# Two subtractions of the last pair's gate inputs move from GpSimd to VectorE

## The chip, the core and the metric

The kernel runs on one core of a Trainium2 chip. A core has a matrix engine (TensorE, PE in the profile; its weight loads are PEld), a vector engine (VectorE, DVE), an engine for activation functions (ScalarE, ACT), a general engine (GpSimd, POOL) and one that only issues transfers (SyncE, SP). Each works through its own instructions in the order in which they were written, and waits on semaphores for the others. Operands lie in SBUF; matmuls write their sums to the eight banks of PSUM, which the other engines read. The metric is the device time of one execution, in microseconds (us).

## What is computed

A gated graph layer on 32 graphs of 512 nodes with 256 features in float32. Cut to what matters here:

```python
h = relu(layernorm(x))
x_conv = relu(bn2(conv17(relu(bn1(conv1(h))))) + h)      # 17 taps along the nodes
x_nmp = (exp(-dist(s)) * adj) @ relu(h @ w_msg + b_msg)  # s: three features of h
gi = concat(x_conv, x_nmp) @ w_ih.T + b_ih
gh = h @ w_hh.T + b_hh
r, z = sigmoid(gi_r + gh_r), sigmoid(gi_z + gh_z)
n = tanh(gi_n + r * gh_n)
out = x + (1 - z) * n + z * h
```

So the three gates r, z and n need three products each, by h, by x_nmp and by x_conv (the sums of r and z can be made in one bank; those of n need h apart from the other two).

## The kernel before

The kernel first makes h, the convolution (by way of a transform along the nodes, with products in the transformed domain) and the messages x_nmp, and leaves them in DRAM. The change lies in the last stage, the gates, from about 815 us of the span on. The loop of this stage goes over 16 pairs of graphs, p = 0 to 15. The order of all instructions on all engines is that of the code (a manual schedule), so what the code writes first on an engine runs first on it.

**Operands of a pair.** HN[p] holds h and x_nmp of both graphs as [128, 2, 4, 512]: two sources and four rows, a row being one half of the features of one graph. CP[p] holds the convolution's rows as [128, 4, 512]; `inverse(p)` (line 870) makes it by PE (line 878), DVE (line 884) and ACT (line 886). The text says "hn" for the first two sources and "c" for the convolution.

**Products.** The gates' matrix products are made by schemes that trade products for sums, so PE is fed with differences of rows. For pairs 0 to 14 the gates r and z go by a scheme of 26 products of 256 columns (`gates_rz26`, line 889, matmuls on line 915), and n by one of seven products of 512 columns (`gate_n`, line 1048). For the last pair, 15, r and z too go by seven products (`gates_rz`, line 939, for r; `last_z`, line 984, for z). All matmuls of the schemes of seven are on line 932. Seven products are named Q1 to Q7 and stand in the order Q1, Q6, Q2, Q7, Q5, Q4, Q3. Each takes one operand:

```python
[plain[B11], r5, plain[B21], t3, t4, r6, plain[B22]]     # Q1, Q6, Q2, Q7, Q5, Q4, Q3 take 0, 1, 2, 3, 4, 5, 6
```

with t4 = row 1 - row 0, r5 = row 3 - t4, t3 = row 3 - row 1, r6 = row 2 - r5 (`PAIR_SUMS`). Each of these has two hn parts (tiles tn, line 812, two instructions) and a c part (tile tnc, line 814, one instruction of 128 x 512). Q6 thus multiplies r5: first its two hn parts, then its c part.

**Where the differences are made.** They are made by GpSimd in `block_sum` (line 795), except for two c parts of the first pair, t4 and r5, which VectorE makes. For the last pair, `sums(15, True)` (line 820) lists t4, r5, t3, r6, each hn before c, and is called behind `gate_n(14)`. On GpSimd they stand behind four weight sums of `load_last` (line 844).

**gate_n and what follows it on VectorE.** In `gate_n(14)`, `finished` (line 1063) reads a product's banks and makes the input of a tanh by four steps of VectorE (lines 1071 to 1074), and `blend` (line 1138) makes the gated result by three steps of VectorE: h - n (reads PSUM), times z (both inputs in SBUF), plus n (reads PSUM). In the profile the steps of the first blend have line 1102, of the second line 1110 and of the last two line 1061. Near its end `gate_n` reads:

```python
        finished(x3, u3, x1, 1, 1)
        pair(Q4, x2, False)
        finished(x2, p1, x2, 1, 0)
        if not last:
            for step in blend(p, 1, 1):
                step()
        pair(Q3, x3, False)
        late = finished(x3, u2, x3, 0, 1, not last)
```

Then comes the last pair's `gates_rz`. ScalarE copies Q1's bank (p1, line 957), VectorE adds it to Q6's bank (u2, line 962), Q7 is added by PE onto that same bank, and VectorE makes u3 from it (line 971); the results come from line 950. The third and fourth blend of pair 14 stand between these.

Of the kernel before, what the change touches and what calls it, by code (L numbers as in the profile page):

```python
# [91 lines left out]
FIRST_ORDER = (  # L92
    ('t4', 'hn'), ('r5', 'hn'), ('E5', 'hn'), ('t3', 'hn'), ('E9', 'hn'), ('E4', 'hn'), ('E8',
    'hn'), ('E0', 'hn'), ('E6', 'hn'), ('t4', 'c'), ('r5', 'c'), ('E5', 'c'), ('t3', 'c'), ('E9',
    'c'), ('E4', 'c'), ('E8', 'c'), ('E0', 'c'), ('E6', 'c'), ('E7', 'hn'), ('E7', 'c'), ('E2',
    'hn'), ('E2', 'c'), ('r6', 'hn'), ('r6', 'c'), ('E1', 'hn'), ('E1', 'c'), ('E3', 'hn'), ('E3',
    'c'),
)
HALFWAY = 12
WEIGHT_SUMS = (  # L100
    '3=a+b', '9=a-c', '4=b+9', '5=d-4', '19=a+g', '6=b+19', '8=h+6', '11=f+9', '20=e+g', '26=f+h',
# [61 lines left out]
def gnn_layer(  # L163
# [15 lines left out]
    nc = tc.nc  # L179
    B, N, D = x.shape  # L180
# [21 lines left out]
    def bank(name):  # L202
        return psum.tile([P, N], FP, tag="bank", name=name)
# [502 lines left out]
    def combine_weights():  # L706

        steps, loads, begins = [], [], []
        for k, src in enumerate((w_hhT, w_ihT[D:], w_ihT[:D])):
# [26 lines left out]
            for n, (dst, x1, x2, op) in enumerate(((Q5, n21, n22, ALU.add), (Q6, q[Q5], n11, ALU.subtract),  # L736
# [4 lines left out]
                if n == 1:  # L741
                    steps[-1].append(partial(nc.sync.dma_start, WH[:, k, :HALFWAY], u[:, :HALFWAY]))
                if n == 0 and k > 0:
                    begins.append(len(steps) - 1)
            steps[-1].append(partial(nc.sync.dma_start, WN[:, k], t))
            steps[-1].append(partial(nc.sync.dma_start, WH[:, k, HALFWAY:], u[:, HALFWAY : len(PRODUCTS)]))
        steps[0].append(loads[0])
# [14 lines left out]
    def shared(name):  # L762
        return pools["yn"].tile([P, 2, len(spans) + 1, D], FP, tag="yn", name=name, bufs=1)
# [14 lines left out]
    def operand(p, name, part):  # L778

        if name[0] == "b":  # L780
            row, cols = place(name)
            return CP[p][:, row, cols] if part == "c" else HN[p][:, :, row, cols]
        if name[0] == "E":
            n = EXTRA.index(name)
            return TEC[0][:, n] if part == "c" else TE[0][:, n]
        row, h = list(PAIR_SUMS).index(name[:2]), int(name[3])
        cols = slice(HALF * h, HALF * h + HALF)
        return TNC[0][:, row, cols] if part == "c" else TN[0][:, row, :, cols]
# [3 lines left out]
                               (TEC, "tec", [len(EXTRA), HALF]), (RZ, "rz", [2 * DC, 2, N]), (CT, "ct", [6, N])):  # L792
            t[0] = pools[name].tile([P, *shape], FP, tag=name, name=name, bufs=1)

    def block_sum(p, name, part):
        if name in BLOCK_SUMS:
            x, op, y = BLOCK_SUMS[name]
            dst, x, y = (operand(p, v, part) for v in (name, x, y))
            op = ALU.add if op == "+" else ALU.subtract
        else:  # L800
            rows = list(PAIR_SUMS)

            def whole(v):
                if isinstance(v, int):
                    return CP[p][:, v] if part == "c" else HN[p][:, :, v]
                return TNC[0][:, rows.index(v)] if part == "c" else TN[0][:, rows.index(v)]

            (x, y), op = PAIR_SUMS[name], ALU.subtract
            dst, x, y = whole(name), whole(x), whole(y)
            if part == "hn":  # L810
                for k in range(2):
                    nc.gpsimd.tensor_tensor(dst[:, k], x[:, k], y[:, k], op=op)  # L812
                return
        (nc.vector if p == 0 and (name, part) in FIRST_ORDER[ahead : ahead + 2] else nc.gpsimd).tensor_tensor(dst, x, y, op=op)

    def sums_ahead(p, part):
        for name in SUMS_AHEAD:
            block_sum(p, name, part)

    def sums(p, last):  # L820
        for name, part in [(name, part) for name in PAIR_SUMS for part in ("hn", "c")] if last else SUM_ORDER:
            block_sum(p, name, part)

    def load_combined(s0, s1):
        if "hk" not in SW:
# [23 lines left out]
    def load_pair_x(p):  # L849

        XP[p] = []
        for b in (2 * p, 2 * p + 1):
            t = pools["xb"].tile([P, N // 32, D // 4], FP, tag="x", name=f"xb_{b}", bufs=2)
            for g in range(4):
                nc.sync.dma_start(t[32 * g : 32 * (g + 1)], quarter(x[b], g))
            XP[p].append(t)
# [72 lines left out]
    def into(bk, q, o, ks, terms, first, t=slice(0, N)):  # L929

        for i, k in enumerate(ks):
            nc.tensor.matmul(bk[:, t], weight(q, k, o), terms[k][q][:, t], start=(first and i == 0), stop=(i == len(ks) - 1),  # L932
                             skip_group_check=True)

    def temp(role, name):
        n = TURN[role] = TURN.get(role, 1) + 1
        return CT[0][:, 2 * ("u3", "p1", "u2").index(role) + n % 2, :]
# [110 lines left out]
    def gate_n(p, terms, last, old=None):  # L1048
        rz, o = RZ[0], 2
        t = shared(f"nt_{p}").rearrange("p j c d -> p (j c d)")  # L1050
        NT[p] = nt = t[:, : DC * 2 * N].rearrange("p (i j n) -> p i j n", i=DC, j=2)
        h, i_ = [0], [1, 2]
        add, mul = ALU.add, ALU.mult

        def pair(q, banks, first):
            for bk, ks in zip(banks, (h, i_)):
                into(bk, q, o, ks, terms, first)

        def run(steps):
            for step in steps:  # L1060
                step()

        def finished(banks, other, spare, i, j, later=False):

            n, r = nt[:, i, j, :], rz[:, i, j, :]
            (bk, bk_i), (h, g) = banks, spare
            if other is None:
                nc.vector.scalar_tensor_tensor(n, bk, b_hn[:, i : i + 1], r, op0=add, op1=mul)
                nc.vector.tensor_add(n, n, bk_i)
            else:  # L1070
                nc.vector.scalar_tensor_tensor(h, bk, b_hn[:, i : i + 1], other[0], op0=add, op1=add)
                nc.vector.tensor_mul(n, h, r)
                nc.vector.tensor_add(g, other[1], bk_i)
                nc.vector.tensor_add(n, n, g)  # L1074
            NEW[p, i, j] = n if last else g
            tanh = partial(nc.scalar.activation, NEW[p, i, j], n, AF.Tanh, bias=b_in[:, i : i + 1], scale=1.0)
            return tanh if later else tanh()  # L1077

        if last:
            old(0)  # L1080
        x1 = [bank(f"pn1_{p}_{k}") for k in range(2)]
        pair(Q1, x1, True)
        p1 = [temp("p1", f"n{p}_{k}") for k in range(2)]
        for k in range(2):
            nc.scalar.copy(p1[k], x1[k])
        x2 = [bank(f"pn2_{p}_{k}") for k in range(2)]
        pair(Q6, x2, True)
        u2 = [temp("u2", f"n{p}_{k}") for k in range(2)]
        for k in range(2):
            nc.vector.tensor_add(u2[k], p1[k], x2[k])  # L1090
        if last:
            old(1)
            load_pair_x(p)
        pair(Q2, x1, False)
        finished(x1, None, x1, 0, 0)
        pair(Q7, x2, False)
        u3 = [temp("u3", f"n{p}_{k}") for k in range(2)]
        for k in range(2):
            nc.vector.tensor_add(u3[k], p1[k], x2[k])
        if not last:  # L1100
            for step in blend(p, 0, 0):
                step()
        x3 = [bank(f"pn3_{p}_{k}") for k in range(2)]
        pair(Q5, x3, True)
        finished(x3, u3, x1, 1, 1)
        pair(Q4, x2, False)
        finished(x2, p1, x2, 1, 0)
        if not last:
            for step in blend(p, 1, 1):
                step()  # L1110
# [3 lines that stand above are left out]
            rest = partial(run, blend(p, 1, 0)), partial(run, blend(p, 0, 1))  # L1114
            if p + 2 < B // 2:
                rest[0]()
                rest = rest[1:]
            return late, *rest
        if last:
            for i, j in ((0, 0), (1, 1), (1, 0), (0, 1)):  # L1120
                nc.gpsimd.tensor_tensor(rz[:, i, j, :], HN[p][:, 0, 2 * i + j, :], nt[:, i, j, :], op=ALU.subtract)
                if j == 0:
                    early_out(p, i, j)
# [14 lines left out]
    def blend(p, i, j):  # L1138
        n, d = NEW.pop((p, i, j)), RZ[0][:, i, j, :]
        return [partial(nc.vector.tensor_tensor, d, HN[p][:, 0, 2 * i + j, :], n, op=ALU.subtract),  # L1140
                partial(nc.vector.tensor_tensor, d, d, RZ[0][:, DC + i, j, :], op=ALU.mult),
                partial(nc.vector.tensor_tensor, NT[p][:, i, j, :], d, n, op=ALU.add)]
# [322 lines left out]
    with phase(*homes), tc.manual_schedule():  # L1465
# [8 lines left out]
        ahead = [v[1] for v in FIRST_ORDER].index("c")  # L1474
        for name, part in FIRST_ORDER[:ahead]:
            block_sum(0, name, part)
# [3 lines left out]
        for p in range(pairs):  # L1480
# [7 lines left out]
            if more:  # L1488
                last = p + 2 == pairs
# [63 lines left out]
```

## Time and profile before

| What | Value |
|---|---|
| median of 4 runs | 1732.99 us (1730.87 to 1736.97) |
| profiled execution, its own time | 1731.53 us |
| its span, first to last instruction | 1729.8 us |
| TensorE busy | 1715.0 us, 99% |
| VectorE busy | 1303.5 us, 75% |
| GpSimd busy | 1085.7 us, 63% |
| mean granted clock of TensorE | 0.999 |

The rows of a timeline are: start in us from the span's start, length in us, engine, line, operation, tile written <- tiles read, shapes, count; in brackets the engine's idle time before it and what ended it. A row with x4 merges four instructions. A float32 matmul shows as two rows on PE, so a 512-column product with three terms has six: four for its hn terms and two for its c term. The name pg is a bank of the r and z gates, pn of the n gate, pz of the last pair's z gate; ct is the tile of the temporaries p1, u2 and u3, rz holds r and z, nt the n gate.

### The profile page before, as it was taken

The page shows a single profiled execution, that of the slowest core. Times are in us where ns is not written, and L with a number is a line of the kernel's source. Part 1 is how long each engine was busy: PE and PEld are TensorE (multiplying, and loading weights), DVE is VectorE, ACT ScalarE, POOL GpSimd, SP SyncE. Part 2 cuts the span into 40 slices and gives each one's busy share as a digit, 9 for nine tenths or more (in the row PEclk, how much of TensorE's full clock was granted, in tenths as well). Part 3 has the DMA queues.
Part 4 walks back from the last instruction along what each step waited for, and adds up shares of the span by engine and source line. Part 5 has one row for each costly group of instructions (what it writes and reads, how often), then busy time and mean ns, then how long its engine had stood idle before and what let it go on. Part 6 is the DMA issues. An engine that isn't in the chain of part 4 may idle for free.

```text
span 1729.8 us, 24317 instructions
## 1 busy us (share of the span) xinstructions
PE 1715.0 (99%) x7920; PEld 1320.4 (76%) x7920; DVE 1303.5 (75%) x2599; ACT 691.4 (40%) x1669; POOL 1085.7 (63%) x1074
## 2 busy tenths in 40 slices
PE   9999999999999999999999999999999999999998
PEld 6767888888998888887877778777877787778744
DVE  7875877777996677666587778777887778777867
ACT  4556655553446555554323232232323232323221
POOL 3331777687655677777767657665667556755551
PEclk9999999999999999999999999999999999999999
DMA  9989988885778888798433454335523553335433
GB/s 260 297 281 259 264 234 243 253 232 178 269 250 230 267 242 244 230 257 305 119 103 74 80 128 112 75 71 128 128 69 64 124 128 88 78 90 128 108 57 73
DMA packets 311681, 295.07 MB, mean 171 GB/s; under 512 B 147436, under 2 KB 241164, under 8 KB 311172
## 3 DMA queue, kind: packets, MB, share of 16 engines
q1 hardware_dynamic: 301588, 265.17, 56.4%
q0 software_dynamic: 6960, 26.65, 4.8%
q10 hardware_dynamic: 3008, 1.72, 0.3%
q8 instruction: 63, 1.03, 0.3%
q14 instruction: 62, 0.51, 0.1%
HBM read 194.31 MB, written 99.16 MB: 170 GB/s over the span
## 4 chain that ended last, share of the span: by engine, by line
PE 89%; DVE 4%; DMA 2%; SPq 2%; issue 1%; POOL 1%; ACT 0%; DVEq 0%; POOLq 0%
PE pg L915 27%; PE pn L932 15%; PE py L503 11%; PE pn L670 10%; PE pm L558 6%; PE pc L439 5%; PE pc L878 3%; PE px L454 3%; PE pd L608 2%; PE phT L419 1%; PE pw L363 1%; PE pz L932 1%; PE pg L932 1%; PE pn L653 1%; PE pc L881 1%
## 5 line engine op out<-in xcount | busy, mean ns | idle before, releaser
L470 POOL TENSOR_TENSOR wsum<-wt 128x512 f32<-128x512 f32 x66 | 94.1, 1426 | 101.6 <-DMA wt<-wd 67.3
L503 PE MATMUL py<-wt,xf 128*128 128x256 f32 x640 | 154.2, 384 | 0.0
L915 PE MATMUL pg<-te,sw 128*128 128x256 f32 x600 | 154.0, 379 | 0.0
L906 ACT ACTIVATE rz<-rz,brz 128x256 f32<-128x256 f32 x180 | 86.2, 504 | 147.0 <-DVE rz L921 146.9
L503 PEld LDWEIGHTS py<-wt,xf 128*128 128x128 f32 x640 | 117.1, 190 | 34.9 <-issue 20.5
L915 PEld LDWEIGHTS pg<-te,sw 128*128 128x128 f32 x600 | 114.0, 190 | 15.5
L915 PE MATMUL pg<-hn,sw 128*128 128x256 f32 x480 | 123.2, 379 | 0.0
L915 PE MATMUL pg<-tn,sw 128*128 128x256 f32 x480 | 123.2, 379 | 0.0
L618 DVE TENSOR_TENSOR A<-A,at 128x512 f32<-128x512 f32 x124 | 115.9, 974 | 6.3 <-ACT A L614 2.7
L932 PE MATMUL pn<-tn,sw_n 128*128 128x512 f32 x256 | 120.3, 592 | 0.0
L1077 ACT ACTIVATE pn<-nt,vech 128x512 f32<-128x512 f32 x45 | 31.1, 692 | 218.7 <-DVE nt L1074 139.4
L439 PE MATMUL pc<-w,hT 128*128 128x256 f32 x512 | 117.7, 383 | 0.7 <-DVE hT L423 0.7
L558 PE MATMUL pm<-wmsg,hq 128*128 128x259 f32 x512 | 117.3, 381 | 0.0
L439 PEld LDWEIGHTS pc<-w,hT 128*128 128x128 f32 x512 | 94.6, 190 | 23.8 <-issue 6.4
L812 POOL TENSOR_TENSOR tn<-hn 128x512 f32<-128x512 f32 x64 | 86.3, 1369 | 35.7 <-PE pn L932 35.6
L558 PEld LDWEIGHTS pm<-wmsg,hq 128*128 128x128 f32 x512 | 96.5, 189 | 14.6
L915 PEld LDWEIGHTS pg<-hn,sw 128*128 128x128 f32 x480 | 91.1, 190 | 18.3 <-PE pn L932 3.3
L915 PEld LDWEIGHTS pg<-tn,sw 128*128 128x128 f32 x480 | 91.2, 190 | 12.4
L921 DVE TENSOR_TENSOR ct<-pg,ct 128x256 f32<-128x256 f32 x180 | 74.8, 415 | 32.9 <-PE pg L915 23.5
L932 PEld LDWEIGHTS pn<-tn,sw_n 128*128 128x128 f32 x256 | 48.6, 190 | 61.2 <-issue 50.9
L932 PE MATMUL pn<-hn,sw_n 128*128 128x512 f32 x192 | 90.3, 592 | 0.0
L915 PE MATMUL pg<-tec,sw 128*128 128x256 f32 x300 | 89.2, 379 | 0.0
(236 smaller groups left out, 4328.0 us busy)
## 6 DMA issues: line engine op xcount, KB each, us to landing
wt<-wd SPq DMA_DIRECT2D x80, 512.0 KB, 6.5
adj<-in_adj_dram SPq DMA_DIRECT2D x128, 256.0 KB, 5.9
wd<-wst SPq DMA_DIRECT2D x64, 320.0 KB, 5.3
yd<-y SPq DMA_DIRECT2D x76, 256.0 KB, 5.0
hd<-hT SPq DMA_DIRECT2D x32, 512.0 KB, 4.7
nd<-nmp SPq DMA_DIRECT2D x32, 512.0 KB, 2.9
xb<-in_x_dram SPq DMA_DIRECT2D x128, 128.0 KB, 6.4
out_dram<-xb SPq DMA_DIRECT2D x122, 128.0 KB, 2.8
```

The source lines that it names most:

```text
L439: nc.tensor.matmul(p[:, j, :], HT[b][:, ic, c * P : (c + 1) * P], w1[:, ic, :], start=(ic == 0), stop=(ic == DC - 1))
L454: nc.tensor.matmul(p[:, j * 2 * L : (j + 1) * 2 * L], H1[b][:, c0 + j, ic * P : (ic + 1) * P], fwd, start=True, stop=True)
L470: nc.gpsimd.tensor_tensor(t, WT[g, u][:, 0], WT[g, u][:, 1], op=ALU.add)
L503: nc.tensor.matmul(dst, v[:, ic, :], w[:, ic, :], start=(ic == 0), stop=(ic == DC - 1))
L558: nc.tensor.matmul(p[:, : D + NS], hq[:, ic, c * P : (c + 1) * P], wmsg[:, ic, :], start=(ic == 0), stop=(ic == DC - 1))
L618: nc.vector.tensor_mul(A[b][:, mc, :], EXP.pop((b, mc)), AT.pop((b, mc)))
L670: nc.tensor.matmul(bk, left[:, k, :], right[:, k, :], start=(first and k == 0), stop=(k == 1), skip_group_check=True)
L812: nc.gpsimd.tensor_tensor(dst[:, k], x[:, k], y[:, k], op=op)
L906: nc.scalar.activation(at(dst), at(src), AF.Sigmoid, bias=brz[:, o : o + 1], scale=sign)
L915: nc.tensor.matmul(bk, SW["hk"][:, k, s, :], c if k == 2 else hn[:, k], start=(onto is None and k == 0), stop=(k == K3 - 1), skip_group_ch ...
L921: nc.vector.tensor_tensor(at(dst), at(x), at(y), op=op)
L932: nc.tensor.matmul(bk[:, t], weight(q, k, o), terms[k][q][:, t], start=(first and i == 0), stop=(i == len(ks) - 1), skip_group_check=True)
```

## The change

The c parts of t4 and r5 of the last pair are made by VectorE instead of GpSimd. They are issued in `gate_n(14)`, behind the `finished` of Q4 and ahead of the second blend (line 1110). `sums(15, True)` leaves them out. The hn parts, t3 and r6 stay on GpSimd in their order.

```diff
+EARLY_SUMS = (("t4", "c"), ("r5", "c"))
...
-    def block_sum(p, name, part):
+    def block_sum(p, name, part, engine=nc.gpsimd):
...
-        (nc.vector if p == 0 and (name, part) in FIRST_ORDER[ahead : ahead + 2] else nc.gpsimd).tensor_tensor(dst, x, y, op=op)
+        if p == 0 and (name, part) in FIRST_ORDER[ahead : ahead + 2]:
+            engine = nc.vector
+        engine.tensor_tensor(dst, x, y, op=op)
...
     def sums(p, last):
         for name, part in [(name, part) for name in PAIR_SUMS for part in ("hn", "c")] if last else SUM_ORDER:
-            block_sum(p, name, part)
+            if not last or (name, part) not in EARLY_SUMS:
+                block_sum(p, name, part)
...
         finished(x2, p1, x2, 1, 0)
+        if p + 2 == B // 2:
+            for name, part in EARLY_SUMS:
+                block_sum(p + 1, name, part, nc.vector)
         if not last:
             for step in blend(p, 1, 1):
```

The instructions of PE, ACT and SP keep their number and order. Three waits change their engine: PE's matmul of r5's c part waits for VectorE instead of GpSimd, VectorE's first difference waits for GpSimd's last reading of the old tnc, and GpSimd's c part of r6 waits for VectorE's r5.

## The prediction, made before the result was known

> **What bounds the kernel now.** I read the page first, then the chain of waits over the last 130 us, then the timelines of TensorE (PE), GpSimd (POOL) and VectorE (DVE) around the point where that chain enters PE. On the page PE is busy for 99% of the span and has 89% of the chain that ended last:
>
> ```profile
> PE 1715.0 (99%) x7920; PEld 1320.4 (76%) x7920; DVE 1303.5 (75%) x2599; ACT 691.4 (40%) x1669; POOL 1085.7 (63%) x1074
> ...
> PE 89%; DVE 4%; DMA 2%; SPq 2%; issue 1%; POOL 1%; ACT 0%; DVEq 0%; POOLq 0%
> ```
>
> The chain of waits shows what PE's last stretch waited for. Columns are start, length, what:
>
> ```profile
> 1669.50 1.73 POOL tnc L814
> 1671.23 0.04 issue
> 1671.28 14.00 PE pg L932 x32
> 1685.28 18.02 PE pn L932 x42
> ```
>
> A POOL subtraction into tnc releases PE at 1671.28, and from there PE works to its last matmul without a break (14.00, 18.02 and then 14.18 us of pz). So a shift of PE after this point is a shift of the end, one for one. The subtraction is r5's convolution part, the second of the two that the change moves. The timeline of PE shows the size of the wait:
>
> ```profile
> 1668.89 1.88 PE L932 MATMUL pg<-tn,sw_last 128*128 128x512 f32 x4
> 1671.28 1.13 PE L932 MATMUL pg<-tnc,sw_last 128*128 128x512 f32 x2 [0.51 <-POOL tnc L814]
> 1672.24 1.88 PE L932 MATMUL pg<-hn,sw_last 128*128 128x512 f32 x4
> ...
> 1674.81 1.88 PE L932 MATMUL pg<-tn,sw_last 128*128 128x512 f32 x4
> ```
>
> The first two rows are product Q6 of the last pair's reset gate (starts 1668.89), the third begins Q2, the fourth Q7. Q2 takes 1674.81 - 1672.24 = 2.57 us, as every 512-column product here does; Q6 takes 1672.24 - 1668.89 = 3.35. The excess, **0.78 us, is all that can be won** from this wait. It also gives the cost of a restart: the subtraction ended at 1671.22, and Q2 began 1.02 later where two matmuls need 0.86 (two thirds of 2.57), so a released product goes on as if it had started 0.16 after its release.
>
> **What the change removes.** POOL loses two 128x512 subtractions. Its rows now are t4 hn (1663.35), t4 c, r5 hn, r5 c:
>
> ```profile
> 1665.81 1.27 POOL L814 TENSOR_TENSOR tnc<-cp 128x512 f32<-128x512 f32 x1
> 1667.05 2.49 POOL L812 TENSOR_TENSOR tn<-hn,tn 128x512 f32<-128x512 f32 x2
> 1669.50 1.72 POOL L814 TENSOR_TENSOR tnc<-cp,tnc 128x512 f32<-128x512 f32 x1
> ```
>
> Without t4 c, r5 hn starts at 1665.81 and ends near 1668.30; Q6's first two terms, wanted by 1668.89 and 1669.75, are then in time, and the small weight-load delay at 1669.59 goes too. t3 and r6, which follow, come earlier than now, and now they are not waited for. POOL's work after them (L1121) starts only at 1695.98, after 16.94 us of idle, so what POOL saves there is worth nothing. No DMA moves, and the queues of SP and ACT keep their order.
>
> **What it adds.** DVE gets t4 c and r5 c behind the four steps that end at 1667.80 and ahead of the second blend. These are the rows behind which they go in, and the one that counts:
>
> ```profile
> 1667.80 0.68 DVE L1110 TENSOR_TENSOR rz<-hn,pn 128x512 f32<-128x512 f32 x1
> 1668.51 1.58 DVE L1110 TENSOR_TENSOR rz<-rz 128x512 f32<-128x512 f32 x1
> 1670.12 0.69 DVE L1110 TENSOR_TENSOR nt<-rz,pn 128x512 f32<-128x512 f32 x1
> ...
> 1673.45 0.68 DVE L962 TENSOR_TENSOR ct<-ct,pg 128x512 f32<-128x512 f32 x1
> ```
>
> L962 (u2) reads the bank of Q6 before Q7 adds onto it, so Q7 waits for L962. Between 1667.80 and L962 DVE has no idle time, so every delay there reaches L962. It ends at 1674.13; Q7 could then have gone on from 1674.29 and starts at 1674.81. **The slack is 0.52 us**: even with no delay of DVE, only 0.52 of the 0.78 would be won. With a delay d of DVE, Q7 moves by d - 0.52.
>
> How long are the two? Both inputs lie in SBUF, and such instructions take 0.70 us alone (rz<-rz at 1674.76) but 1.58 and 1.63 (1660.09) while POOL works. The same two subtractions stand once on DVE in this trace, for the first pair. The first took 0.70 (from 821.13), the second this:
>
> ```profile
> 822.01 1.50 DVE L814 TENSOR_TENSOR tnc<-cp,tnc 128x512 f32<-128x512 f32 x1 [0.18 <-ACT cp L886]
> ```
>
> The timeline of POOL beside it:
>
> ```profile
> 821.36 1.61 POOL L814 TENSOR_TENSOR te<-te,hn 128x512 f32<-128x512 f32 x1
> 822.92 1.71 POOL L814 TENSOR_TENSOR te<-hn,te 128x512 f32<-128x512 f32 x1
> ```
>
> They take turns: POOL's instruction ends at 822.97, DVE's 0.54 after it, at 823.51; POOL's next, 1.27 when alone, takes 1.71. Around 1668.51 it is the same: POOL ends at 1669.54, DVE at 1670.09 (0.55 later), POOL at 1671.22 (1.13 later). With 0.55 and 1.13 the new order is: t4 c issues at 1667.80, POOL's r5 hn ends at 1668.30, t4 c ends at 1668.85. POOL, waiting by then, takes its turn until 1669.98, and r5 c ends at 1670.53. POOL ends again at 1671.66. The blend's first step reads PSUM and isn't held (0.68), its second, issued near 1671.2, ends at 1671.66 + 0.55 = 1672.21, where it ends at 1670.09 now. **d = 2.1.** r5 c itself is just in time: Q6 wants it at 1670.61 and may go on from 1670.69.
>
> Sum: u2 ends at 1676.25, Q7 goes on from 1676.41 instead of 1674.81: **+1.6 us**, the wait of 0.78 replaced by one of about 2.2. Nothing behind it takes it back, as PE has no break after it; nothing adds to it, since u3 (L971) now waits 1.40 for PE and the L950 rows 1.8 and more, in which DVE catches up.
>
> Bounds: at least 1.22 for the two (0.61 apart, as 1670.12 to the next start at 1670.73) less 0.88 (the blend's 1.58 falling to 0.70), d = 0.34, **-0.2**; at most 1.63 each with no relief, d = 3.26, **+2.7**. I take 1.6, by the rows nearest in place and kind.
>
> On the Trainium skill, "SBUF — State Buffer", "Practical consequences": a VectorE instruction with two SBUF inputs and a GpSimd instruction that reads SBUF block each other fully, the second starting when the first has finished. Taken word for word, each turn would cost its full length (0.70 and 1.27), and the sum would be an estimated +2.3. The rows hand over earlier than that (0.55 and 1.13), so I keep 1.6.
>
> **The rivals.**
> - *Faster, about -0.5.* The two instructions cost DVE nothing net, so u2 isn't late and only its 0.52 counts. It decides where d is below 0.5. For it: the wait of 0.51 is real and the lower bound reaches it. Against: two instructions of 0.6 in a row of DVE without idle time, and the first pair's 1.50. Median about 1732.5.
> - *The difference is not ready earlier, so the change doesn't do what it says.* If POOL gets one turn more between the two (1.27), r5 c ends at 1671.8, later than POOL's 1671.22; Q6's wait stays, and Q7's comes on top: +2.9, median 1735.9. Against: each hand-over in the rows is one instruction for one.
> - *Slower by the clock.* PE would stand for some 2.2 us. The granted clock was 1.00 after the longest break in this trace (1.13 us, at 7.69), and it falls from 1.00 to a mean of 0.85 in 1724 to 1726 and 0.50 after, 3 to 5 us behind the last matmul. Between 1.13 and 4 nothing is shown. The price from the first matmuls: 20 records of 128x128 took 4.19 us (from 1.48), the next 8 of that shape 1.06; 20 at the latter rate are 2.65, so 1.5 lost. +3.1, median 1736.1. It decides only if the break is long enough to drop the clock.
>
> For that last one the Trainium skill, "TensorE: Matmul & The Clock Gate", Part 1, speaks against: the clock drops after an idle window of about 3.4 us. By it the price at 2.2 us is nothing; by the rows alone it stays open.
>
> **How the numbers follow.** The profiled execution took 1731.53 us, 1.73 more than its span of 1729.8. By the sum the span becomes 1731.4 and that execution 1733.1. It lies 1.46 under the median of the four runs, 1732.99; the change is counted onto the median: 1732.99 + 1.6 = **1734.6**. Chances: forecast (between -0.2 and +2.7) 0.73, faster 0.08, not ready 0.11, clock 0.05, none of these 0.03. No case reaches 0.3% (5.2 us), about what a measurement of this kernel can tell from no change; not even the last two together (+4.4). What goes beyond it would be scatter (the four runs lie 6.1 apart): same 0.93, slower 0.05, faster 0.02. Range: 1732.99 - 0.5 - 1.2 = 1731.3 to 1732.99 + 2.9 + 1.1 = 1737.0, the ends being the rivals with about a us of scatter of a median.
>
> **What would show it.** In the changed kernel's timeline: Q6 no longer held by POOL; t4 c and r5 c on DVE near 1667.8, some 1.1 and 1.6 long; u2 starting near 1675.6 instead of 1673.45; and PE waiting some 2.2 us ahead of Q7, on DVE. The forecast is wrong if u2 starts within 0.5 us of its old place, if Q6 still waits, or if matmuls after Q7's wait are further apart than 0.43.

## The result, and the profile after

| | before | after |
|---|---|---|
| median of all its runs | 1731.84 us (52 runs) | 1733.55 us (34 runs) |
| profiled execution, own time | 1731.53 us | 1734.2 us |
| its span | 1729.8 us | 1732.4 us |

The ratio is 1.0012, with a 95% interval of 1.0007 to 1.0016: the changed kernel is slower by 1.2 to 2.8 us. The forecast was 1734.6 us, 1.6 us above the median then known.

The page of the changed kernel: busy times first, then the shares of the chain of waits by engine. Line numbers of after lie 1 to 7 higher than those of before (L814 is L817, L932 is L936, L962 is L966, L1110 is L1117).

```profile
PE 1714.8 (99%) x7920; PEld 1320.6 (76%) x7920; DVE 1303.8 (75%) x2601; ACT 691.3 (40%) x1669; POOL 1083.9 (63%) x1072
...
PE 93%; DVE 3%; DMA 1%; issue 1%; POOL 1%; ACT 0%; SPq 0%; ACTq 0%; DVEq 0%; POOLq 0%
```

Two instructions went from POOL to DVE (x1074 to x1072, x2599 to x2601). PE's busy time is what it was (1715.0 before), in a span 2.6 us longer: what was added is waiting. Where it is, the chain of waits of after shows (start, length, what):

```profile
1668.21 0.69 DVE nt L1078
1668.90 1.00 DVE tnc L817
1669.93 1.64 DVE tnc L817
1671.57 0.61 DVE rz L1117
...
1676.61 0.69 DVE ct L966
1677.30 0.14 issue
1677.44 10.54 PE pg L936 x24
1687.98 18.03 PE pn L936 x42
1706.00 14.18 PE pz L936 x36
```

Before, the chain entered PE from POOL's subtraction, with 32 matmuls of pg still to come; now it comes through DVE, over the two moved subtractions and the blend to u2 (L966), and enters with 24 left. Behind it the same unbroken PE as before. PE's timeline of after:

```profile
1667.82 1.88 PE L936 MATMUL pg<-hn,sw_last 128*128 128x512 f32 x4
...
1670.39 1.88 PE L936 MATMUL pg<-tn,sw_last 128*128 128x512 f32 x4
1672.11 1.02 PE L936 MATMUL pg<-tnc,sw_last 128*128 128x512 f32 x2
1672.96 1.88 PE L936 MATMUL pg<-hn,sw_last 128*128 128x512 f32 x4
1674.68 1.02 PE L936 MATMUL pg<-cp,sw_last 128*128 128x512 f32 x2
1677.44 1.95 PE L936 MATMUL pg<-tn,sw_last 128*128 128x512 f32 x4 [1.74 <-DVE ct L966]
```

Q1 starts at 1667.82, Q6 at 1670.39, Q2 at 1672.96, Q7 at 1677.44. Q6 takes 2.57 us, no longer 3.35. Q7 begins 4.48 us after Q2, where 2.57 would do: a stop of 1.9 (1.74 of it idle). And DVE's timeline of after:

```profile
1668.82 1.07 DVE L817 TENSOR_TENSOR tnc<-cp 128x512 f32<-128x512 f32 x1
1669.93 1.64 DVE L817 TENSOR_TENSOR tnc<-cp,tnc 128x512 f32<-128x512 f32 x1
1671.49 0.68 DVE L1117 TENSOR_TENSOR rz<-hn,pn 128x512 f32<-128x512 f32 x1
1672.20 1.05 DVE L1117 TENSOR_TENSOR rz<-rz 128x512 f32<-128x512 f32 x1
...
1676.61 0.68 DVE L966 TENSOR_TENSOR ct<-ct,pg 128x512 f32<-128x512 f32 x1
```

From the place where the two go in to u2's start were 1673.45 - 1667.80 = 5.65 us before; now they are 1676.61 - 1668.82 = 7.79. **d = 2.14**, forecast 2.1, and each row has about the forecast length (1.07, 1.64, and 1.05 for the blend's second step instead of 1.58).

**A measure that leaves the rest of the execution out.** The two spans differ by 2.6, but 1.5 of that was there before the last pair: PE began the last pair's `inverse(15)` at 1643.56 before and at 1645.08 after, and the other profiles lie between 1641.87 and 1644.57 there. So the stretches are compared from here on. M runs from Q1's first matmul to the first of pz: 14 products, 14 x 2.575 = 36.05 us if PE never stops. N runs from `inverse(15)`'s first matmul to the same end (58.78 was the shortest seen). Before: M 36.83, N 59.58. After: M 38.02, N 60.75. The change costs **+1.19 in M** and +1.17 in N, just below the interval's lower end of 1.2.

M has two places for a stop, Q6 and Q7, and the later one counts only for what it exceeds the earlier. Q7 without a stop starts 7.725 after Q1 and goes on 0.16 after u2's end, u2 being 0.68 long. This is the theory, as one rule:

M = 36.05 + the larger of (Q6's wait) and (u2's start after Q1, less 6.885).

Before: the larger of 0.78 and 7.14 - 6.885 = 0.26, so 36.83. After: Q6 0, u2 8.79 - 6.885 = 1.91, so 37.96 (38.02 measured). Rivals to it: that the price lies in sharing SBUF and not in the order on VectorE; that a granted clock falls in the new stop; that it is a scatter of the profile.

### The profile page after: what moved, and what is told of

Same layout as the page of the kernel before. It is cut to its first block, busy times and chain, and to the rows that moved or that the text cites. A ratio compares the mean times of both kernels' runs of the same rounds, so it can differ in the third digit from the quotient of the medians.

```text
span 1732.4 us, 24314 instructions
## 1 busy us (share of the span) xinstructions
PE 1714.8 (99%) x7920; PEld 1320.6 (76%) x7920; DVE 1303.8 (75%) x2601; ACT 691.3 (40%) x1669; POOL 1083.9 (63%) x1072
## 3 DMA queue, kind: packets, MB, share of 16 engines
q10 hardware_dynamic: 3008, 1.72, 0.3%
q8 instruction: 63, 1.03, 0.2%
## 4 chain that ended last, share of the span: by engine, by line
PE 93%; DVE 3%; DMA 1%; issue 1%; POOL 1%; ACT 0%; SPq 0%; ACTq 0%; DVEq 0%; POOLq 0%
PE pg L919 29%; PE pn L936 16%; PE py L504 11%; PE pn L671 10%; PE pm L559 6%; PE pc L440 6%; PE pc L882 4%; PE px L455 3%; PE pd L609 2%; PE pw L364 1%; PE phT L420 1%; PE pz L936 1%; PE pc L885 1%; PE pn L654 1%; PE pg L936 1%
## 5 line engine op out<-in xcount | busy, mean ns | idle before, releaser
L936 PE MATMUL pn<-tn,sw_n 128*128 128x512 f32 x256 | 120.3, 592 | 0.0
L936 PEld LDWEIGHTS pn<-tn,sw_n 128*128 128x128 f32 x256 | 48.6, 190 | 61.2 <-issue 50.9
L936 PE MATMUL pn<-hn,sw_n 128*128 128x512 f32 x192 | 90.3, 592 | 0.0
```

## The experiments

The first tells the place on VectorE from the move as such. **e1_early** keeps both subtractions on VectorE, but issues them at the head of `gate_n(14)`, into places of their own (in the tile TEC, unused there), since tnc is still being read. The lines that lead the products to these places are left out here:

```diff
...
+        if p + 2 == B // 2:
+            for name, part in EARLY_SUMS:
+                block_sum(p + 1, name, part, nc.vector)
         x1 = [bank(f"pn1_{p}_{k}") for k in range(2)]
...
         finished(x2, p1, x2, 1, 0)
-        if p + 2 == B // 2:
-            for name, part in EARLY_SUMS:
-                block_sum(p + 1, name, part, nc.vector)
```

> The two c parts are made by VectorE at the head of gate_n(14), in its idle time before the first u2 step (2.75 us, GpSimd idle too), into two free rows of another tile, so that no reader of the old values is waited for. Measure: M, from the start of the last pair's Q1 (first pg of line 932 or its like) to the start of the first pz. Before 36.83 us, after the change 38.02, and 14 products of 2.575 without any stop are 36.05. Theory (the change loses because its two instructions delay u2; Q6's wait itself is worth 0.78): Q6's wait goes, u2 keeps its place, M between 36.05 and 36.4, and the time 0.4 to 0.8 us below the kernel before, 1.6 to 2 below the change. Rival (the loss of the change lies elsewhere, in the 1.5 us that its profiled run had lost before this stretch): M falls as well but the time stays 1 to 2 us above the kernel before.

VectorE's timeline of e1_early at the new place:

```profile
1648.85 0.68 DVE L823 TENSOR_TENSOR tec<-cp 128x512 f32<-128x512 f32 x1
1649.72 0.69 DVE L823 TENSOR_TENSOR tec<-cp,tec 128x512 f32<-128x512 f32 x1 [0.19 <-ACT cp L898]
1651.68 0.69 DVE L1105 TENSOR_TENSOR ct<-ct,pn 128x512 f32<-128x512 f32 x1 [1.27 <-PE pn L944]
```

They take 0.68 and 0.69, and DVE still waits 1.27 for PE behind them: here they cost nothing. u2 starts 7.13 after Q1 (before 7.14), Q6 doesn't wait, and M is 36.36 (rule 36.30). So the price of the change goes with the place. GpSimd is idle there too, so this run alone doesn't part the order on VectorE from the sharing with GpSimd; the next does. Against before e1_early is level, and the 0.4 to 0.8 us expected below it didn't show: 1730.58 against 1730.60 us, ratio 1.0000 (0.9991 to 1.0009). N tells where the 0.47 of M went: it is 59.68, not shorter than before's 59.58, as a stop ahead of Q3 of pair 14 grew by 0.57. There the first blend's second step took 2.19 us beside GpSimd's weight sums (1.63 before).

**e4_defer** leaves the subtractions where the change puts them, and takes the second blend out of u2's way instead: the last three blends of pair 14 each move one place later, the second behind u2, the third behind u3, the fourth behind the first result.

```diff
...
+        between(2)
...
-        if not last:
+        if not last and p + 2 < B // 2:
             for step in blend(p, 1, 1):
...
+            else:
+                rest = partial(run, blend(p, 1, 1)), *rest
...
-                for step in (late[:2], (), late[2:])[i + 1]:
+                for step in (late[:2], (), late[2:3], late[3:])[i + 1]:
```

> The change as it is, and the last three blends of pair 14 each moved one place later: the second behind u2, the third behind u3, the fourth behind the first result. VectorE has three steps less ahead of u2. Theory: the two differences stay where they are and take as long (about 1.1 and 1.6 us), but u2 comes about 2.7 us earlier than in the change, so Q7 does not wait: M 36.05 to 36.3 and the time 0.4 to 0.8 us below before. Rival (the two instructions cost by taking the shared access to SBUF from GpSimd or by anything other than u2's place): M stays near 38.

Timelines of VectorE, then of PE, in e4_defer:

```profile
1667.45 1.07 DVE L817 TENSOR_TENSOR tnc<-cp 128x512 f32<-128x512 f32 x1
1668.55 1.65 DVE L817 TENSOR_TENSOR tnc<-cp,tnc 128x512 f32<-128x512 f32 x1
1670.12 0.75 DVE L1076 SCALAR_TENSOR_TENSOR pn<-pn,vech,ct 128x512 f32<-128x512 f32 x1
...
1672.84 0.68 DVE L966 TENSOR_TENSOR ct<-ct,pg 128x512 f32<-128x512 f32 x1
```

```profile
1670.26 1.12 PE L936 MATMUL pg<-tnc,sw_last 128*128 128x512 f32 x2
1671.22 1.88 PE L936 MATMUL pg<-hn,sw_last 128*128 128x512 f32 x4
1672.93 1.02 PE L936 MATMUL pg<-cp,sw_last 128*128 128x512 f32 x2
1673.79 1.88 PE L936 MATMUL pg<-tn,sw_last 128*128 128x512 f32 x4
```

The subtractions are as long as in after (1.07, 1.65), and yet the stop ahead of Q7 is gone: Q7 follows Q2 by 2.57. M is 36.15, the 0.10 lying at Q6's c part (1.12 instead of 1.02). So a slow subtraction is harmless where what stands behind it still comes in time. Here u2 just does: it starts 6.87 after Q1, and 6.885 is the latest that costs nothing. N is 59.40, only 0.18 below before, as a stop of some 0.5 stands ahead of pair 14's Q3 here too. Time 1730.82 us, ratio to before 0.9998 (0.999 to 1.0007): level again, and the gain expected isn't shown.

**e9_early_defer** joins the edits of e1_early and e4_defer.

> Both of the two edits before: differences at the head of gate_n(14) and the blends one place later. Theory: neither Q6 nor Q7 waits, M 36.05 to 36.1, time 0.8 us below before. Rival (something else holds PE next): M over 36.3.

VectorE's timeline of e9_early_defer at u2 and behind it:

```profile
1671.07 0.69 DVE L974 TENSOR_TENSOR ct<-ct,pg 128x512 f32<-128x512 f32 x1 [1.44 <-PE pg L944]
1671.67 0.68 DVE L1074 TENSOR_TENSOR rz<-hn,pn 128x512 f32<-128x512 f32 x1
1672.39 2.87 DVE L1074 TENSOR_TENSOR rz<-rz 128x512 f32<-128x512 f32 x1
```

DVE now waits 1.44 for PE at u2, the reverse of after, and M is 36.05: no stop at all. N is 58.78, 0.8 below before. The time is 1729.96 us, ratio to before 0.9994 (0.9986 to 1.0003). A second sample of it was run beside a second one of the changed kernel, on the same chip.

> The version with the differences at the head of gate_n(14) and the blends one place later, timed once more beside the change, on one chip. Theory: M 36.05 again, about 0.8 us below before and 2 below the change. Rival: the interval of the first comparison (0.9986 to 1.0003) was luck, and it stands level with before.

> The change itself, beside the version before it on the same chip. Theory: M 37.9 to 38.5 in any profile, 1 to 2 us above before.

e9_again: M 36.05, N 58.78 again; 1730.70 us against 1731.16 of before, 0.9997 (0.9989 to 1.0006). after_again: M 37.99, N 60.73; 1733.00 us, 1.0015 (1.0006 to 1.0024). The stop of after is thus no scatter of one profile, and its price was seen twice in the time. Between after and e9 lie 2.3 us here. Against before, e9 is 0.5 to 0.6 us below in medians both times, and both intervals hold 1: a gain isn't shown.

**e2_no_t3r6** takes away what makes VectorE share SBUF. GpSimd's t3 and r6 of the last pair are not made.

```diff
-        for name, part in [(name, part) for name in PAIR_SUMS for part in ("hn", "c")] if last else SUM_ORDER:
+        for name, part in [(name, part) for name in ("t4", "r5") for part in ("hn", "c")] if last else SUM_ORDER:
```

> The change, with GpSimd's t3 and r6 of the last pair left out (its products take the values of the pair before, so the last pair's output is not the reference's). GpSimd then is idle behind r5's hn parts, and only t4 c still meets it. Theory (half of d is GpSimd's turns): t4 c 1.05 us, r5 c 0.70, the blend's second step 0.70, d = 0.8, M about 37.1 (36.6 to 37.1, as VectorE reached the place 0.5 earlier against PE in the profiled run of the change than in that before). Rival (the turns do not matter, only two more instructions): M 38.0.

VectorE's timeline of e2_no_t3r6:

```profile
1667.43 1.06 DVE L817 TENSOR_TENSOR tnc<-cp 128x512 f32<-128x512 f32 x1
1668.53 0.69 DVE L817 TENSOR_TENSOR tnc<-cp,tnc 128x512 f32<-128x512 f32 x1
...
1669.85 0.69 DVE L1117 TENSOR_TENSOR rz<-rz 128x512 f32<-128x512 f32 x1
...
1673.90 0.68 DVE L966 TENSOR_TENSOR ct<-ct,pg 128x512 f32<-128x512 f32 x1
```

t4 c still meets r5 hn (1.06); r5 c falls from 1.64 to 0.69 and the blend's step from 1.05 to 0.69. M is 36.99, the rule's value for u2 at 7.82. From the place where the two go in to u2's start it takes 1673.90 - 1667.43 = 6.47, so d is 0.82 instead of 2.14: 1.32 of d is sharing SBUF with t3, and 0.82 is the order on VectorE, with GpSimd out of the way but for r5 hn. M shows only 1.03 of the 1.32, since VectorE reached the place 1.35 after Q1 here and 1.00 in after. Its one time was 1731.35 us (before 1731.08).

**e8_t4_only** moves only t4 c and leaves r5 c on GpSimd.

```diff
-EARLY_SUMS = (("t4", "c"), ("r5", "c"))
+EARLY_SUMS = (("t4", "c"),)
```

> Half of the change: only t4's c part is made by VectorE, r5's stays on GpSimd behind its hn parts. Theory: t4 c takes about 1.05 us on VectorE but the blend behind it is held 0.6 less, d = 0.45, which is inside the slack of 0.52; r5 c ends near 1670.0 on GpSimd's side, in time for Q6. M 36.05 to 36.75, time 0 to 0.8 us below before. Rival (each instruction costs its length, half of the change's loss): M 37.0 to 37.4.

Timelines of GpSimd, then PE, of e8_t4_only:

```profile
1669.39 1.72 POOL L817 TENSOR_TENSOR tnc<-cp,tnc 128x512 f32<-128x512 f32 x1
```

```profile
1671.16 1.12 PE L936 MATMUL pg<-tnc,sw_last 128*128 128x512 f32 x2 [0.55 <-POOL tnc L817]
```

M was 37.02, above what was expected: Q6 waits 0.97 for GpSimd, longer than in before (0.78), where nothing had been moved. The reason lies earlier, in GpSimd's phase, that is, how far its work runs ahead of PE's: GpSimd began t4's hn part 1.99 us before Q1, where it was 2.96 in before and 3.44 in after, so that a whole instruction less was still too late. The SyncE queue had issued the transfer of the weights 0.73 us later (1646.87, before 1646.14; counted from Q1, 1.03 later), and GpSimd's four sums, which wait for them, started 9.80 ahead of Q1 instead of 10.61. Time 1731.34 us, 1.0004 (0.9995 to 1.0013). The same kernel was run again, to see whether the phase does it.

> Half of the change once more, one look. In its first profile u2 was in time, as expected, but Q6 waited for r5 c, since GpSimd began the four weight sums 9.80 us ahead of Q1 instead of 10.61 before (the weights had landed later). Theory: M follows the start of GpSimd's sums: about 36.1 to 36.3 where they begin 10.6 us or more ahead of Q1, 37.0 where 9.8. Rival (half of the change costs by itself): 37.0 in either case.

With t4's hn part 2.96 ahead of Q1, as in before, Q6 no longer waits. PE's timeline of e8_again:

```profile
1668.92 1.02 PE L936 MATMUL pg<-tnc,sw_last 128*128 128x512 f32 x2
...
1673.34 1.96 PE L936 MATMUL pg<-tn,sw_last 128*128 128x512 f32 x4 [0.81 <-DVE ct L966]
```

M is 37.10, though, and not the 36.1 to 36.3 expected, for u2 is late: t4 c took 1.07 and the blend's step 1.33, so that d was 0.74 instead of 0.45. The rule with u2 at 7.88 gives 37.04. One kernel, then, has its stop at Q6 in one execution and at Q7 in the next.

**e5_defer_alone** is the kernel before with e4_defer's edit of the blend only; both subtractions stay on GpSimd.

> The kernel before with only the last three blends of pair 14 one place later. Theory: u2 has slack before the change, so taking work away ahead of it is worth nothing, Q6's wait for GpSimd stays: M 36.7 to 36.9. Rival (the order of the blends earns by itself what the version with both edits showed): M 36.1 to 36.4.

M is 36.05: a miss of the expectation, which had Q6's wait stay. GpSimd's timeline of e5_defer_alone:

```profile
1665.41 1.28 POOL L814 TENSOR_TENSOR tnc<-cp 128x512 f32<-128x512 f32 x1
1666.63 2.50 POOL L812 TENSOR_TENSOR tn<-hn,tn 128x512 f32<-128x512 f32 x2
1669.09 1.27 POOL L814 TENSOR_TENSOR tnc<-cp,tnc 128x512 f32<-128x512 f32 x1
```

r5 c ends 3.53 after Q1 (which starts at 1666.83), in before 4.91. Of these 1.38 us, 0.45 are the blend's turn (1.27 instead of 1.72), and 0.92 are GpSimd's phase, t4's hn part starting 3.88 ahead of Q1 instead of 2.96. By before's phase a wait of some 0.3 would be left (an estimate: 0.78 - 0.45). How much each would do in a mean over executions isn't settled. Its one time was 1731.21 us.

**e7_double** doubles the suspected cost: behind the two subtractions VectorE makes them again, into two other places that nobody reads.

```diff
                 block_sum(p + 1, name, part, nc.vector)
+            spares = [TEC[0][:, n : n + 2].rearrange("p a n -> p (a n)") for n in (0, 2)]
+            nc.vector.tensor_tensor(spares[0], CP[p + 1][:, 1], CP[p + 1][:, 0], op=ALU.subtract)
+            nc.vector.tensor_tensor(spares[1], CP[p + 1][:, 3], spares[0], op=ALU.subtract)
```

> The change, and the same two subtractions once more behind themselves, into unused rows. Theory: four turns with GpSimd in place of two, 1.68 us each, d = 5.5, M 41.3 to 41.8, PE standing for about 5 us ahead of Q7. Clock rival: behind so long a stop the matmuls are further apart than 0.43 us (up to 0.86) for some us and the granted clock shows below 1.00, M 43 or more. If the clock stays at 1.00 in the change (stop of 1.7 to 2) but falls here, the limit lies between.

PE's timeline of e7_double, and below it the windows (length, then busy us and instructions of PE, PEld, DVE, ACT and POOL, then the granted clock):

```profile
1678.22 3.76 PE L936 MATMUL pg<-tn,sw_last 128*128 128x512 f32 x4 [5.44 <-DVE ct L966]
1681.77 1.87 PE L936 MATMUL pg<-tnc,sw_last 128*128 128x512 f32 x2
```

```profile
1673.00:1676.00 3.00, 0.00 (x0) 0.00 (x0) 2.93 (x4) 0.00 (x0) 3.00 (x3) 1.00 0.00 0
1676.00:1678.00 2.00, 0.00 (x0) 0.00 (x0) 1.97 (x5) 0.49 (x1) 0.39 (x1) 0.66 0.00 0
1678.00:1680.00 2.00, 1.78 (x2) 0.84 (x3) 1.93 (x4) 0.81 (x2) 0.00 (x0) 0.50 0.01 4
```

u2 starts 12.59 after Q1, 3.80 later than in after: 3.3 for the two subtractions of 1.75 and 1.63, and 0.49 because VectorE reached the place 1.49 after Q1, in after 1.00. The rule alone gives M 41.76; M was 44.42. The other 2.66 is the clock rival: PE stood for 5.44 us, the granted clock went to 0.50, and four matmuls took 3.76 instead of 1.88. The time was 1737.55 us (before 1731.08). The windows of the changed kernel over its own stop:

```profile
1674.00:1676.00 2.00, 1.70 (x4) 0.40 (x3) 1.94 (x3) 0.00 (x0) 2.00 (x3) 1.00 0.00 0
1676.00:1678.00 2.00, 0.56 (x2) 0.35 (x3) 1.96 (x4) 1.27 (x2) 2.00 (x2) 1.00 0.02 4
```

Its clock stays at 1.00, here and in after_again, so in these two executions none of the price is the clock.

**Behind the first blend.** Two more places were tried. e3_behind_first_blend puts the loop behind the first blend, into tnc; in this place pair 14's Q5 multiplies the last pair's t4 instead of its own.

> The two differences on VectorE behind the first blend of pair 14, some 5 us earlier than in the change, still in the stretch in which VectorE has no idle time up to u2. Theory: any place in this stretch costs about the same, from the start of inverse(15) to the first pz 59.58 + 1.2 to 2.7 = 60.8 to 62.3 us (before 59.58, the change 60.76). Rival (it is the place next to the second blend that costs): 59.6 or less.

M was 36.05 but N 63.54: Q5 of pair 14 read what it had to wait for, so the wait is the edit's own and tells nothing of VectorE. Time 1735.1 us. e3b_behind_first_blend has the same place with the rows of its own of e1_early:

```diff
...
                 step()
+        if p + 2 == B // 2:
+            for name, part in EARLY_SUMS:
+                block_sum(p + 1, name, part, nc.vector)
         x3 = [bank(f"pn3_{p}_{k}") for k in range(2)]
...
```

> The two differences behind the first blend of pair 14 as in the run before, but into two free rows of another tile, so that every product takes its right operands and pair 14's Q5 waits for nothing new. Theory (VectorE has no idle time from the first blend to u2, and what is put in delays the first reader behind it that PE waits for): here that is Q3 of pair 14, which waits for the steps of Q5; VectorE is 2.2 to 3.2 us late there, Q6 and Q7 then wait no more, and from the start of inverse(15) to the first pz it takes 61 to 62 us, up to 63.8 if the clock falls in a stop of 3 us (before 59.58, the change 60.75). Rival (only the place ahead of u2 costs): 59.0 to 59.6.

VectorE's timeline of e3b_behind_first_blend, PE's, and the windows:

```profile
1662.86 1.58 DVE L823 TENSOR_TENSOR tec<-cp 128x512 f32<-128x512 f32 x1
1664.48 1.63 DVE L823 TENSOR_TENSOR tec<-cp,tec 128x512 f32<-128x512 f32 x1
```

```profile
1666.84 3.47 PE L944 MATMUL pn<-hn,sw_n 128*128 128x512 f32 x4 [2.21 <-DVE pn L1083]
```

```profile
1666.00:1667.00 1.00, 0.16 (x1) 0.17 (x2) 0.96 (x3) 0.00 (x0) 1.00 (x1) 1.00 0.00 0
1668.00:1670.00 2.00, 2.00 (x3) 0.90 (x3) 1.93 (x4) 0.69 (x1) 2.00 (x3) 0.50 0.00 0
```

M has no stop (36.05), since it moved to an earlier product that waits for VectorE, pair 14's Q3: N is 62.96, 3.4 above before. That stop was 2.21 of idle PE, only 0.47 longer than after's, and the clock fell to 0.50 for 3.41 us, which cost about 1.8 (passes 0.68 to 0.86 apart instead of 0.43). Time 1735.63 us (before 1729.4), one run each.

The kernels by the rule, u2 and Q6's wait as measured in each (e3 and e3b have theirs earlier):

| kernel | u2's start after Q1 | Q6's wait | M by the rule | M | N | t4's hn part ahead of Q1 |
|---|---|---|---|---|---|---|
| before | 7.14 | 0.78 | 36.83 | 36.83 | 59.58 | 2.96 |
| after | 8.79 | 0 | 37.96 | 38.02 | 60.75 | 3.44 |
| after_again | 8.77 | 0 | 37.93 | 37.99 | 60.73 | 3.45 |
| e1_early | 7.13 | 0 | 36.30 | 36.36 | 59.68 | 2.95 |
| e4_defer | 6.87 | 0.10 | 36.15 | 36.15 | 59.40 | 2.96 |
| e9_early_defer | 5.42 | 0 | 36.05 | 36.05 | 58.78 | 3.27 |
| e9_again | 5.42 | 0 | 36.05 | 36.05 | 58.78 | 3.01 |
| e2_no_t3r6 | 7.82 | 0 | 36.99 | 36.99 | 59.72 | 3.10 |
| e8_t4_only | 7.33 | 0.97 | 37.02 | 37.02 | 59.75 | 1.99 |
| e8_again | 7.88 | 0 | 37.04 | 37.10 | 59.84 | 2.96 |
| e5_defer_alone | 5.42 | 0 | 36.05 | 36.05 | 58.78 | 3.88 |
| e7_double | 12.59 | 0 | 41.76 | 44.42 | 67.21 | 2.96 |

Where Q6's wait is the larger, the rule's value is M by definition. The tests are the rows where u2 decides: all within 0.06 but e7_double, whose difference is the clock.

## Why the prediction was right, point by point

- **At most 0.78 to win, and Q6 in time: right.** Q6 takes 2.57 in both profiles of after. But 0.78 was the value of one execution. In e8_t4_only Q6 waited 0.97 even with one subtraction less on GpSimd, in e5_defer_alone not at all with both. The wait hangs on GpSimd's start too, which spread from 1.99 to 3.88 ahead of Q1 over these kernels (1.99 and 2.96 in two executions of the same one, e8_t4_only). The prediction took it for fixed.
- **The slack of u2, and the restart 0.16 after a release: right** within 0.06 over the rows above.
- **The two subtractions some 1.1 and 1.6 long, d = 2.1: right** (1.07, 1.64, 2.14). Turns with GpSimd and the order on VectorE share it: without t3's turns d is 0.82, and M still 0.94 above 36.05.
- **The sum of +1.6: the mechanism right, the size too high by 0.4** in the stretch (+1.19). The term that failed is the place where the two go in. It was taken as fixed against PE, 1.49 after Q1; in after it was 1668.82 - 1667.82 = 1.00. VectorE came there 0.49 earlier, as the first blend's second step had taken 1.13 instead of 1.63 beside a GpSimd that began its weight sums 11.10 ahead of Q1 instead of 10.61. So PE stood idle for 1.74 ahead of Q7 where 2.2 was forecast. With before's 1.49 the rule gives u2 at 9.28 and M 38.45, an estimate of +1.6 as forecast. d wasn't touched by this, since GpSimd's work too lay 0.49 further ahead (3.44 instead of 2.96) and met VectorE as forecast.
- **The time: +1.6 forecast, 1.2 to 2.8 measured.** The profiled stretch gives 1.2. Whether a mean execution loses more than the two profiled ones isn't known: the medians of after and before stand 1.7 apart, and the phase moves single executions by some tenths of a us. That 1.7 lies so near 1.6 is thus no proof of the sum. The forecast median of 1734.6 was 1.05 too high because its base was: 1732.99 from four runs, 1731.84 from 52. And 0.3% was named as about what can be told from no change; with this many runs the interval is 0.09% wide, and a change of 0.12% is clear of it.
- **Faster by 0.5: fell**, for d was 2.1 and not below 0.5. e1_early shows its condition, a place where the two cost nothing, and even there N was no shorter than before.
- **Not ready earlier: fell**; r5 c ended at 1671.57, 3.75 after Q1, and Q6 didn't wait. The reason given against it, one instruction for one at each hand-over, doesn't hold always: in e9_early_defer a step of VectorE missed a turn (2.87 us).
- **Slower by the clock: ruled out for the two profiled executions, by little, and open for others.** There was no fall at 1.74 and 1.71 us of idle, and one at 2.21 in e3b. The price of 1.5 was near what e3b showed (1.8). With before's phase the stop of the change would be some 2.2 us too. Five of its 34 runs took 1736.6 to 1738.0 us (one of the 52 of before took over 1736.5), at a mean granted clock of 0.996 or 0.997, where the profiled execution has 0.999 and e7_double 0.997. No trace of these five is kept, so whether the clock fell there in the new stop isn't known.

That the time grows because u2 stands behind the moved work is shown: taking the blend away (e4_defer), moving the subtractions away (e1_early) and doubling them (e7_double) moved Q7 as the rule has it, but for the clock in e7_double. Not settled is how GpSimd's phase and the blend's turn share the absence of Q6's wait in e5_defer_alone, and whether e9 is truly faster than before. Its N is 0.8 us shorter, as much as the change set out to remove, but that is 0.05% of the time and below what samples of eleven runs resolve.

## What to carry to other kernels

Before a wait is taken off one engine by work on another, look for the next instruction on that other engine which the bottleneck waits for, and give its slack a number: 0.52 us of slack against 2.1 us of new work decided this case. If the work must go there, put it where the engine waits anyway (e1_early), or move behind the due instruction what nobody needs yet (e4_defer). A wait of less than a us read from one profile may be a matter of that execution's phase: before counting it as a gain, ask what started the chain ahead of it.

## What the runs showed of the hardware

- **Sharing SBUF goes by turns.** VectorE's two-input subtraction of 128x512 took 0.69 with GpSimd silent and 1.06 to 1.75 beside it, GpSimd's 1.27 and 1.72. The turns aren't always one for one: in e9_early_defer the blend's product, issued at 1672.39, went past GpSimd's end at 1673.49 and ended 0.54 behind the next, at 1674.72, after 2.87 us.
- **The clock falls after shorter breaks than expected.** 1.74 us of idle PE left the granted clock at 1.00, 2.21 us brought it to 0.50 for 3.41 us (e3b), 2.89 for 3.41 (e3), 5.44 for 6.83 (e7_double). The Trainium skill, "TensorE: Matmul & The Clock Gate", Part 1, gives an idle window of about 3.4 us as what drops the clock. Here a break of two thirds of that was enough, and the measurement decides; the length of the slow time, 3.41 or twice that, is near its window. In the clock records of the traces every stretch between two changes is a whole number of 3.413 us (1720.32 in before is 504 of them), so changes fall on a grid. Counted back from the changes, an estimate, the most idle time in one step of it was 1.38 and 1.71 us in the two traces of the change and 2.21 and 2.75 in e3b and e3. So how a break lies in this grid could decide too; no run tests it.
- **A transfer's landing moves a wait far from it.** The weights issued 0.73 us later in e8_t4_only came back as a wait at Q6, some 20 us on and on another engine.
